# Two-layer cross-attention on one core: layer 2's keys and queries in two and a half blocks, and row maxima turned by one product

## The chip, the cores and the metric

The kernel runs on one core of a Trainium2 chip. The metric is the device time of one execution in microseconds (us): 1476.69 us is the median of three runs before the change (1475.23, 1476.69 and 1477.35 us).

The engines are named as in the profile. PE is the matrix engine, and PEld its weight load: each product loads a stationary operand and then streams a moving one past it. DVE is the vector engine, ACT the scalar engine, POOL the general engine, SP the engine that issues most of the transfers (DMAs). Each executes its own list of instructions in order; semaphores make one wait for another.

## The reference

Two layers follow each other on 16 batches of 256 positions with 320 channels, each with 20 heads of 16 channels. The context of a batch has 256 rows of 512 channels. Layer 1 takes its first 77 rows as text and the other 179 as image tokens; layer 2 takes the last 4 as image tokens and the other 252 as text. Cut to layer 2:

```python
q = heads(hidden_states @ W_q)
k_t = heads(text_ehs @ W_k)
scores_t = jnp.einsum('bhsd,bhtd->bhst', q, k_t) * attn_scale
probs_t = jax.nn.softmax(scores_t, axis=-1)
text_out = jnp.einsum('bhst,bhtd->bhsd', probs_t, v_t)
...
k_ip = heads(ip_ehs @ W_k_ip)
attn_scores = jnp.einsum('bhsd,bhnd->bhsn', q, k_ip) * attn_scale
qsem = jnp.einsum('bhst,bte->bhse', probs_t, text_ehs)
qsem = _l2norm(qsem)
sem = jnp.einsum('bhse,bne->bhsn', qsem, ip_n)
fused = attn_scores + SEM_SCALE * sem
probs_ip = jax.nn.softmax(fused, axis=-1)
probs_ip = probs_ip * spatial_mask[None, None, :, None]
ip_out = jnp.einsum('bhsn,bhnd->bhsd', probs_ip, v_ip)
...
out = out @ W_out + b_out
out = out + residual
```

`ip_n` are the normalised image tokens. All inputs and results are 32-bit floats.

## The kernel before, in words

**Halves.** PE multiplies in a rounded 32-bit type. To keep the accuracy, an operand is held as a high half (rounded, by ACT) and a low half (the remainder, by DVE or POOL), and a product is the sum of high by high, high by low and low by high: three products for each block of 128 contracted rows (`prod`). Queries contract 320 rows, two and a half blocks, with the half block's halves side by side in one block, so `project` has 8 products where a full count would be 9.

**Heads in 24 places.** The weights of queries and keys have their columns ordered by channel and head, 16 times 24 = 384 columns (`CP`), of which 20 of each 24 are heads. Layer 1 packs them to 320 (`CQ`). Layer 2 keeps 384: three whole blocks of 128 columns. `keys1` makes the keys of one batch, block by block (`m`), each with 4 x 3 products of 252 columns; `queries` with `project` makes the queries, each block with 8 products of 256 columns.

**Stacks.** Halves of keys and queries go through a scratch tensor in memory, `kd` and `qd`, with three copies of each channel row: keys low, high, high and queries high, low, high. `stacks1` loads, for each group of four heads, 48 rows (three copies of 16 channels) into `ks` and `qs`, two heads side by side in the upper and two in the lower half of the partitions, so that one product of 48 rows gives a score with all its halves. A 49th row of `ks` holds -1, and the same row of `qs` the row maximum, so the second, turned product gives the score less its maximum.

**Slots.** The work of one group of four heads is a slot: 80 slots of layer 1 (`slot0`), then 80 of layer 2 (`slot1`), five to a batch. In slot k of layer 2 `both1` is called for t = 0 and 1: the turned scores of group k into the banks T (line 917), the plain scores of group k+2 into bank S (line 922), the row maxima of these on DVE (line 923), and ACT's exponentials (line 929). Between the two, `attend1` makes the values' products of group k-2 into the single bank P (lines 988 and 990), which `settle1` reads; `norm1` makes the quadratic forms of group k-1 (line 975, the costliest group), and `rounded1` the halves of the probabilities (lines 965 and 966).

**Row maxima.** The maxima lie with positions on partitions, and are needed as a row. `maxima1` (line 955) and `maxima0` of layer 1 (line 780) turn them by two products with the unit matrix, one for each 128 positions, into a bank of the ring X. ACT copies the 4 or 8 rows of 256 numbers to `mt` (lines 957 and 782), and a DMA issued by ACT (line 959) carries them into the stacks. In layer 2 this stands at the end of slot k for group k+2.

**What sets the order.** A table, `STEPS`, says at which time, in slots, each step of the other work (keys "k1", queries "o1", tokens "t1", closing "c1" and "i1", weights "w1" to "w8") is put between the parts of the slots: `fill(k + part)` runs the steps that are due. PE's order is that of the calls throughout; in layer 2 that of ACT, DVE and POOL too. SP's order, and in layer 1 that of the others, is made by a scheduler from its own estimate of the times. `late` holds DVE's remainders and the DMAs behind them back between `hold` (before the last part of a slot) and `release` (before the second `both1`).

Of the kernel before, what the change touches and what calls it, by code (L numbers as in the profile page):

```python
# [16 lines left out]
B = 16  # L17
S = 256
# [15 lines left out]
KS1 = 49  # L34
XROW = 48

# [3 lines left out]
LEAD = 4  # L40

# [8 lines left out]
def xattn2(  # L50
# [101 lines left out]
    kd = [dram.tile([B // 2, 3, CQ, 2, S], F32, name="kd0"), dram.tile([B, 3, CP, 1, S], F32, name="kd1")]  # L152
# [81 lines left out]
    def weights(w_d, tag, half=None, wait=0, raw="raw"):  # L234

        w, parts, view = by_row(w_d, tag)
        yield from in_turn(parts, wait, raw)
        if half is not None:
            nc.vector.tensor_scalar_mul(w[:, 1, 2], f(w[:, 1, 2]), half)
        return view  # L240

# [105 lines left out]
    def keys_out(d, m, kst, b=slice(None)):  # L347

        for r, s in ((slice(1, 3), 0), (slice(0, 1), 1)):
# [130 lines left out]
    def weights7():  # L480
        cip = w1["cip"]
        image, wki1 = by_column(wki1_d)
        _, text, w1["k"] = by_row(wk1_d, "wA")
        yield from in_turn(image + text, 0.3, "rawc")
        for m in range(3):
            kp = bank()[:, :BI]
            prod(kp, lambda s, k: wki1(s, k, slice(m * 128, m * 128 + 128)), lambda s, k: cip[:, s, k], 4)
            halves(kip[:, 0, m], kip[:, 1, m], kp)
            yield

    def weights6():
# [15 lines left out]
        for i in range(2):  # L507
# [4 lines left out]
            v1t.append(v)  # L512
        yield

    def weights2():
        wq.append((yield from weights(wq1_d, "wE", tmask[:, 3:4], 0.3, "rawc")))
# [36 lines left out]
    def keys1(b):  # L553
        ct = ct1[b] = yield from context(b, 1, 0.3)
        for m in range(3):
# [4 lines left out]
            prod(kp, lambda s, k: w1["k"](s, k, ms), lambda s, k: ct(s, k)[:, :T1], 4)  # L560
# [4 lines left out]
                lambda kst=kst, m=m: keys_out(kd[1][b], m, kst),  # L565
# [60 lines left out]
    def project(l, w, a, evac):  # L626
# [9 lines left out]
    def queries(l, a):  # L636
# [6 lines left out]
        yield from project(l, wq[l], a, evac)  # L643
        qd = dram.tile([3, (CQ, CP)[l], S], F32, tag=f"qd{l}", name=f"qd{l}", bufs=2)
# [12 lines left out]
    def stack_rows(d):  # L657
        return d.rearrange("r (d h) t -> (r d) h t", d=D)

# [87 lines left out]
    def stacks1(k):  # L747
# [7 lines left out]
        for u in range(2):  # L755
            rows = slice(64 * u, 64 * u + XROW)
            hs = slice(4 * g + u, 4 * g + u + 3, 2)
            if k - NS < n:
                dma(K[64 * u + XROW : 64 * u + KS1], w1["ind"])
# [710 lines left out]
```

## Time and profile before

| | |
|---|---|
| median of three runs | 1476.69 us (1475.23 to 1477.35) |
| span of the profiled execution | 1475.7 us |
| what the median has beyond that span | 1.0 us (no time of the profiled execution is given apart from its span) |
| PE busy | 1433.6 us (97%), 12438 products |
| PEld busy | 1186.7 us (80%) |
| DVE, POOL, ACT busy | 1166.0, 1151.8, 956.5 us (79%, 78%, 65%) |
| DMA engines, mean busy share in slices | 0.1 to 0.7 |
| granted clock of PE, mean | 0.993 |

In a row of groups stand the line, the engine, the operation, the tiles (written <- read), the shapes and the count, then the busy time of the group, the mean duration of one in ns, and the idle time before them with what ended it. Products overlap: the mean of one (some 280 ns for 256 columns) is longer than what one adds to PE's time, which is the distance from its start to the next one's start. In a timeline row the first number is the start, the second the length in us, and a count at the end says how many instructions the row joins. Layer 1's slots fill the first 670 us or so, and layer 2's the rest.

### The profile page before, as it was taken

Reading aid. Unit: us, or ns where it says so; the run is one execution under the profiler, and the core shown is the slowest. Engines: PE = TensorE matmul, PEld = TensorE weight load, DVE = VectorE, ACT = ScalarE, POOL = GpSimd, SP = SyncE. Lnnn points to the kernel's source line nnn. Section 1 sums busy time; section 2 is a strip of 40 time slices with the busy share of each in tenths; the row PEclk is TensorE's granted clock in tenths of the full one; section 3 lists DMA queues with packets and bytes.
Section 4 is the critical chain, followed back from the end, with each engine's and each line's share of the span. In section 5 each row is a group of like instructions: output and inputs, shape, how many; then the busy total and the mean of one; then the engine's idle time right before and its main releaser. Section 6 shows DMA issues by size and latency. Waiting matters only on the chain.

```text
span 1475.7 us, 35302 instructions
## 1 busy us (share of the span) xinstructions
PE 1433.6 (97%) x12438; PEld 1186.7 (80%) x12438; DVE 1166.0 (79%) x2569; ACT 956.5 (65%) x2074; POOL 1151.8 (78%) x1173
## 2 busy tenths in 40 slices
PE   6899999999999999799999999999999999999998
PEld 6788888888888878687778887888888888888865
DVE  5487676777677787967888888888888888888897
ACT  5577676767676776756666566656665666566553
POOL 4179797979797877987788877787778877887785
PEclk9999999999999999999999999999999999999999
DMA  6756565656656577565434433543354345433511
GB/s 196 194 160 184 134 184 141 184 143 165 162 154 164 144 195 205 140 184 158 138 102 140 146 119 101 161 146 102 118 161 146 89 131 161 135 101 116 150 32 50
DMA packets 230667, 211.78 MB, mean 144 GB/s; under 512 B 56314, under 2 KB 217116, under 8 KB 230492
## 3 DMA queue, kind: packets, MB, share of 16 engines
q1 hardware_dynamic: 229222, 208.56, 50.3%
q8 instruction: 99, 1.62, 0.5%
q10 hardware_dynamic: 1270, 0.98, 0.2%
q14 instruction: 76, 0.62, 0.1%
HBM read 122.07 MB, written 86.44 MB: 141 GB/s over the span
## 4 chain that ended last, share of the span: by engine, by line
PE 86%; DMA 4%; DVE 3%; POOL 3%; ACT 2%; issue 1%; SPq 0%; ACTq 0%; DVEq 0%; POOLq 0%
PE X L260 22%; PE X L975 18%; PE X L632 11%; PE P L833 7%; PE S L772 5%; PE P L988 5%; PE T L917 5%; PE T L795 4%; PE S L922 3%; PE P L990 2%; DMA kd<-kst 2%; PE X L1108 1%; POOL P L801 1%; PE X L690 1%; POOL wt L966 1%
## 5 line engine op out<-in xcount | busy, mean ns | idle before, releaser
L801 POOL TENSOR_TENSOR P<-P,rs 128x512 f32<-128x512 f32 x320 | 413.6, 1316 | 140.2 <-ACT P L798 140.2
L975 PE MATMUL X<-ctb,gm 128*128 128x512 f32 x1120 | 295.3, 407 | 0.0
L966 POOL TENSOR_TENSOR wt<-P,ctb 128x512 f32<-128x512 f32 x212 | 268.6, 1296 | 0.0
L923 DVE TENSOR_REDUCE mn<-S 128x4 fp32r<-128x1008 f32 x160 | 192.8, 1205 | 81.0 <-PE S L922 79.4
L975 PEld LDWEIGHTS X<-ctb,gm 128*128 128x128 f32 x1120 | 203.6, 190 | 49.4 <-issue 0.4
L798 ACT ACTIVATE P<-T 128x512 f32<-128x512 f32 x320 | 174.7, 593 | 100.5 <-PE T L795 81.0
L978 DVE TENSOR_TENSOR wt<-X,wt 128x512 f32<-128x512 f32 x240 | 159.3, 681 | 4.9 <-PE X L975 4.9
L929 ACT ACTIVATE P<-T 128x512 f32<-128x512 f32 x212 | 115.0, 597 | 54.5 <-PE T L917 41.6
L980 POOL TENSOR_TENSOR wt<-wt 128x512 f32<-128x512 f32 x80 | 103.6, 1295 | 58.3 <-DVE wt L978 58.3
L965 ACT ACTIVATE ctb<-P 128x512 fp32r<-128x512 f32 x212 | 122.5, 625 | 32.7 <-PE X L975 31.1
L774 DVE TENSOR_REDUCE mn<-S 128x4 fp32r<-128x716 f32 x160 | 142.4, 890 | 0.0
L833 PE MATMUL P<-P,vr 128*32 128x256 f32 x1920 | 123.8, 387 | 1.8 <-DVE tmp L850 0.8
L632 PE MATMUL X<-hq,wE 128*128 128x256 f32 x768 | 111.1, 289 | 4.4 <-ACT hq L615 3.9
L260 PE MATMUL X<-cta,wA 128*128 128x252 f32 (+3 forms) x726 | 104.2, 289 | 6.9 <-ACT wA L187 6.8
L632 PE MATMUL X<-ho,wF 128*128 128x256 f32 x768 | 106.6, 284 | 0.9 <-DVE ho L871 0.6
L632 PEld LDWEIGHTS X<-hq,wE 128*128 128x128 f32 x768 | 101.6, 195 | 7.2 <-ACT hq L615 4.4
L260 PEld LDWEIGHTS X<-cta,wA 128*128 128x128 f32 (+1 forms) x726 | 94.4, 191 | 10.7 <-ACT wA L187 7.0
L632 PEld LDWEIGHTS X<-ho,wF 128*128 128x128 f32 x768 | 98.7, 189 | 3.9 <-DVE ho L871 1.0
L844 DVE STREAM_TRANSPOSE nt<-P 128x512 f32<-128x512 f32 x80 | 57.0, 713 | 44.2 <-PE P L833 43.9
L773 DVE TENSOR_REDUCE mn<-S 128x4 fp32r<-128x308 f32 x160 | 74.5, 466 | 21.5 <-PE S L772 21.1
L833 PEld LDWEIGHTS P<-P,vr 128*32 128x32 f32 x1920 | 55.7, 110 | 42.7 <-issue 6.0
L772 PE MATMUL S<-ks,qs 125*128 125x256 f32 x480 | 87.0, 304 | 0.9 <-DVE mn L774 0.8
(223 smaller groups left out, 3279.7 us busy)
## 6 DMA issues: line engine op xcount, KB each, us to landing
qd<-q SPq DMA_DIRECT2D x48, 384.0 KB
kd<-kst SPq DMA_DIRECT2D x66, 256.0 KB
rawc<-in_cT_dram SPq DMA_DIRECT2D x60, 256.0 KB
qs<-qd SPq DMA_DIRECT2D x160, 96.0 KB
ks<-kd SPq DMA_DIRECT2D x160, 96.0 KB
qs<-qd SPq DMA_DIRECT2D x60, 192.0 KB
ks<-kd SPq DMA_DIRECT2D x60, 192.0 KB
qd<-q SPq DMA_DIRECT2D x32, 256.0 KB
```

The source lines that it names most:

```text
L260: last = mm(out, lhs(a, k), rhs(b, k), start=i == 0, stop=i == len(terms) - 1)
L632: mm(pp, w(s, k, slice(m * 128, (m + 1) * 128)), a[:, t], start=i == 0, stop=i == len(terms) - 1)
L772: mm(sp[:, h], Q[: XROW + T0, h, t * 128 : (t + 1) * 128], K[: XROW + T0, h], start=True, stop=True)
L774: anchor(nc.vector.tensor_reduce(mn[:, t, 1], sp[:, :, T0:], axis=AX.X, op=ALU.max))
L798: exp = anchor(nc.scalar.activation(pt, st[p], AF.Exp, scale=SCALE))
L801: anchor(nc.gpsimd.tensor_mul(pt, pt, rs[:, t : t + 1].to_broadcast([128, 2, S])))
L833: mm(pv[32 * s : 32 * s + 32, o : o + S], v[:, vt, h : h + 32], P[k, s // 2][:, t, s % 2], start=vt < 2, stop=vt != 1,)
L923: anchor(nc.vector.tensor_reduce(maxes[k + 2][:, t], sp[:, :, :T1], axis=AX.X, op=ALU.max))
L965: nc.scalar.activation(R[k, u][:, t], P[k, u][:, t], AF.Copy, scale=0.5)
L966: anchor(nc.gpsimd.tensor_sub(W[k, u][:, t], P[k, u][:, t], f(R[k, u][:, t])))
L975: mm(yp, gm[:, gb], R[k, u][:, kt], start=i == 0, stop=i == len(blocks[n]) - 1)
L978: nc.vector.tensor_mul(product, yp, w[:, n])
```

## The change

**Layer 2's columns are packed to 320**, so the third block has 64 columns, and the other 64 columns of the block hold the low half of the weights' same columns (`both_halves`, by POOL, once). One product then gives high weights by the moving operand in its upper 64 rows and low weights in its lower 64 rows. Keys: 8 products for the third block in place of 12. Queries: 5 in place of 8. The lower 64 rows are not added to the upper: they are written to the scratch as rows of their own, and the stacks grow from 48 rows to 56 (`XR1`), with the row of -1 at 57. Each head has 8 more rows, of which 4 carry the keys' remainders against the queries' high half, and 4 the other way round; rows without a partner are zero (written once, in `weights6`).

**The scratch writes** are cut accordingly: for a batch 9 DMAs for the keys in place of 6, and 8 for the queries in place of 3. The loads of the stacks stay 4 to a group, of 56 rows in place of 48.

**The row maxima** are stored so that one product turns both halves of the positions: 16 rows of 128 numbers in layer 1, 8 in layer 2, in place of 8 and 4 rows of 256. In layer 2 the step moves from the end of slot k, for group k+2, to the middle of slot k behind the second `both1`, for group k+1, and its product goes into columns 384 to 511 of the values' bank P (77 of 80; three go to a bank of X).

**The image keys' weights** of layer 2 come in four loads by rows in place of three by columns.

**The table** moves to the head of the file; most times stay. "o1" has its fifth time at -5.4 (was -4), and a few times of weights, tokens and closings differ by up to 1.4 slots.

```diff
-KS1 = 49
 XROW = 48
+XR1 = 56
+KS1 = XR1 + 1
+C3 = 2 * 128
...
-        "o1": (-7, -6.8, -6, -5.8, -4, -3.4,),
+    "o1": (-7, -6.8, -6, -5.8, -5.4, -3.4,),
...
+    def both_halves(w):
+
+        for k in range(w.shape[2]):
+            nc.gpsimd.tensor_copy(w[:, 0, k, CQ:], f(w[:, 1, k, C3:CQ]))
...
+    def keys_out1(d, m, kst):
+
+        n = min(128, CQ - m * 128)
+        at = lambda q: slice(q * H + m * 128, q * H + m * 128 + n)
+        twice = d[16 * H : 48 * H].rearrange("(r p) t -> p r t", r=2)[m * 128 : m * 128 + n]
+        dma(twice, kst[:n, 0].unsqueeze(1).to_broadcast([n, 2, S]))
+        dma(d[at(0)], kst[:n, 1])
+        if m:
+            p = 112 * (2 - m)
+            dma(d[52 * H + 16 * (m - 1) : 52 * H + 16 * (m - 1) + n - p], kst[p:n, 0])
+        if m == 2:
+            dma(d[48 * H + 16 : 52 * H], kst[64:, 0])
...
+        none = v1t[0][:16, 0, 512:]
+        for c in range(2):
+            half = slice(128 * c, 128 * c + 128)
+            dma(kd[1][:, 48 * H : 48 * H + 16, half].rearrange("b p t -> p b t"), none.unsqueeze(1).to_broadcast([16, B, 128]))
+            for i in range(2):
+                dma(qd1[i][52 * H : 52 * H + 16, half], none)
...
-            prod(kp, lambda s, k: w1["k"](s, k, ms), lambda s, k: ct(s, k)[:, :T1], 4)
+            if m < 2:
+                prod(kp, lambda s, k: w1["k"](s, k, ms), lambda s, k: ct(s, k)[:, :T1], 4)
+            else:
+                for i in range(8):
+                    mm(kp, w1["k"](0, i // 2, ms), ct(i % 2, i // 2)[:, :T1], start=i == 0, stop=i == 7)
...
+            if packed and m == 2:
+                terms = [(0, 0, 0), (0, 0, 3), (0, 1, 1), (0, 1, 4), (0, 2, 2)]
...
-            for r, s in ((0, 0), (1, 1), (2, 0)):
-                dma(qd[r].rearrange("(m p) t -> p m t", p=128), qh[:, s])
+            whole = lambda q: qd[q * H : q * H + C3].rearrange("(m p) t -> p m t", p=128)
+            for q, s in ((0, 0), (16, 1), (32, 0)):
+                dma(whole(q), qh[:, s, :2])
+            dma(qd[: 48 * H].rearrange("(r p) t -> p r t", r=3)[C3:, ::2], qh[:64, 0, 2].unsqueeze(1).to_broadcast([64, 2, S]))
+            dma(qd[16 * H + C3 : 32 * H], qh[:64, 1, 2])
+            dma(qd[48 * H : 48 * H + 16], qh[112:, 0, 1])
+            dma(qd[48 * H + 16 : 52 * H], qh[:64, 0, 2])
+            dma(qd[52 * H + 16 :], qh[64:, 0, 2])
...
-        mp = bank()
-        for t in range(2):
-            mm(mp[:8, t * 128 : (t + 1) * 128], mn[:, t].rearrange("p a h -> p (a h)"), ident_r, start=True, stop=True)
-        mt = buf("mt", [8, S], FR)
-        casts.append(nc.scalar.copy(mt, mp[:8, :S]))
+        mp = bank()[:16, :128]
+        mm(mp, mn.rearrange("p a h t -> p (a h t)"), ident_r, start=True, stop=True)
+        mt = buf("mt", [16, 128], FR)
+        casts.append(nc.scalar.copy(mt, mp))
...
-    def maxima1(k):
+    def maxima1(k, into=None):
         mn = maxes[k]
-        mp = bank()
-        for t in range(2):
-            mm(mp[:4, t * 128 : (t + 1) * 128], mn[:, t], ident_r, start=True, stop=True)
-        mt = buf("mt", [8, S], FR)[:4]
-        nc.scalar.copy(mt, mp[:4, :S])
-        row = QK[k][0].rearrange("(u p) j t -> u p j t", u=2)[:, XROW]
+        mp = bank()[:8, :128] if into is None else into[:8, 384:]
+        mm(mp, mn.rearrange("p c t -> p (c t)"), ident_r, start=True, stop=True)
+        mt = buf("mt", [8, 128], FR)
+        nc.scalar.copy(mt, mp)
+        row = QK[k][0].rearrange("(u p) j t -> u p j t", u=2)[:, XR1]
         late(lambda: nc.scalar.dma_start(f(row), f(mt)))
...
         yield release
         yield lambda: both1(k, 1)
+        if k > NS:
+            yield lambda: maxima(k + 1, *[x[2] for x in summed])
...
         yield 0.8
-        yield lambda: maxima(k + 2)
         yield lambda: stacks(k + LEAD)
```

Over the whole program the lists differ, in PE, by 64 fewer products of keys (576 of 252 columns become 512), 48 fewer of queries (768 become 720) and 160 fewer of maxima (320 become 160). SP issues 135 more DMAs (1191 become 1326).

PE, one slot of layer 2 from its second `both1` to the next slot's first (T and S are the turned and plain scores, `gm` the operand of the quadratic forms, `hq` that of the queries, `ident_r,mn` the maxima, `wA` the keys). Before:

```order
L917 MATMUL T<-qs_188,ks_192 128x256 x4
L922 MATMUL S<-ks_190,qs_186 128x256 x4
L975 MATMUL X<-ctb_82,gm 128x512 x4
L632 MATMUL X<-hq_293,wE_85 128x256 x8
L975 MATMUL X<-ctb_82,gm 128x512 x3
L975 MATMUL X<-ctb_83,gm 128x512 x7
L955 MATMUL X<-ident_r,mn_555 4x128 x2
L260 MATMUL X<-cta_80,wA_84 128x252 x6
L260 MATMUL X<-cta_81,wA_84 128x252 x6
L917 MATMUL T<-qs_188,ks_192 128x256 x4
L922 MATMUL S<-ks_190,qs_186 128x256 x4
```

And in the changed kernel (line 1018 is what was 917, 1023 was 922, 1055 was 955, 1075 was 975, 725 was 632, 325 was 260):

```order
L1018 MATMUL T<-qs_190,ks_194 128x256 x4
L1023 MATMUL S<-ks_192,qs_188 128x256 x4
L1055 MATMUL P<-ident_r,mn_558 8x128
L1075 MATMUL X<-ctb_84,gm 128x512 x4
L725 MATMUL X<-hq_295,wE_87 128x256 x8
L1075 MATMUL X<-ctb_84,gm 128x512 x3
L1075 MATMUL X<-ctb_85,gm 128x512 x4
L725 MATMUL X<-hq_295,wE_87 128x256 x5
L1075 MATMUL X<-ctb_85,gm 128x512 x3
L325 MATMUL X<-cta_82,wA_86 128x252 x6
L325 MATMUL X<-cta_83,wA_86 128x252 x6
```

The maxima's product stands right behind the plain scores, into bank P, and the third block of the queries, now of 5 products, stands in this slot; before, its 8 products closed the next slot.

SP, the writes and loads of one batch of layer 2 (`kst` and `q` hold the halves of keys and queries, `kd` and `qd` are the scratch, `ks` and `qs` the stacks). Before:

```order
L83 DMA kd_67<-kst_235 128x2x256
L83 DMA kd_67<-kst_235 128x256
L83 DMA out_dram<-xc_747 128x3x256
L83 DMA qd_14293<-q_297 128x3x256 x2
L83 DMA xc_747<-x1d 128x3x256
L83 DMA qd_14293<-q_297 128x3x256
L83 DMA kd_67<-kst_236 128x2x256
L83 DMA kd_67<-kst_236 128x256
L83 DMA qs_188<-qd_14293 48x2x256 x4
L83 DMA qs_186<-qd_14293 48x2x256 x2
L83 DMA kd_67<-kst_235 128x2x256
L83 DMA kd_67<-kst_235 128x256
```

In the changed kernel, from the query loads of the same place on:

```order
L139 DMA qd_0_68<-q_299 64x256 x3
L139 DMA qs_190<-qd_0_68 56x2x256 x4
L139 DMA kd_67<-kst_237 128x2x256
L139 DMA kd_67<-kst_237 128x256
L139 DMA out_dram<-xc_747 128x3x256
L139 DMA xc_747<-x1d 128x3x256
L139 DMA qs_188<-qd_0_68 56x2x256 x2
L139 DMA kd_67<-kst_238 128x2x256
L139 DMA kd_67<-kst_238 128x256
L139 DMA kd_67<-kst_238 16x256
L139 DMA kd_67<-kst_237 64x2x256
L139 DMA kd_67<-kst_237 64x256 x3
```

All eight writes of the queries and the first four query loads now stand ahead of the first block of keys; between the last block of keys (four writes) and the key loads stand two query loads, as before.

ACT, around the maxima of one slot. Before:

```order
L957 CAST mt_196<-X 4x256
L959 DMA qs_187<-mt_196 2x2x256
L929 ACTIVATE P_95<-T 128x512
L929 ACTIVATE P_96<-T 128x512
L929 ACTIVATE P_95<-T 128x512
L929 ACTIVATE P_96<-T 128x512
L615 CAST hq_293<-xq_122 128x768
L965 ACTIVATE ctb_82<-P_95 128x512 x2
```

In the changed kernel (line 1030 was 929, 1065 was 965, 1057 was 957):

```order
L1030 ACTIVATE P_97<-T 128x512
L1030 ACTIVATE P_98<-T 128x512
L1030 ACTIVATE P_97<-T 128x512
L1030 ACTIVATE P_98<-T 128x512
L1057 CAST mt_198<-P 8x128
L1059 DMA qs_188<-mt_198 2x4x128
L1065 ACTIVATE ctb_84<-P_97 128x512 x2
```

The copy and the issue of its DMA moved from ahead of the slot's four exponentials to behind them, ahead of the halves of line 965. DVE's first read of bank P in `settle1` now also waits for this copy by ACT.

More of the change, by code (lines that the diff above doesn't have):

```diff
@@ L634, in project, with queries @@
             yield
-    def queries(l, a):
+    def queries(l, a, b=0):
         qh = buf("q", [128, 2, 3, S], FR)
@@ L995, in slot1 @@
         mine = k < 2 * NS
+        summed = []
         if k == NS:
@@ L1127, in open1 @@
         get("w2")
-        return (yield from queries(1, xs))[1]
+        return (yield from queries(1, xs, b))[1]
     results, tasks, delayed = {}, {}, []
@@ L1276, in ahead, with maxima @@
             both1(k - 2, t)
-    def maxima(k):
+    def maxima(k, *into):
         if k < 2 * NS:
-            (maxima0 if k < NS else maxima1)(k)
+            if k < NS:
+                maxima0(k)
+            else:
+                maxima1(k, *into)
     def part(*key):
```

107 lines of the change are left out of this document (63 added, 44 removed), and 58 rows, old and new, of the table STEPS.

## The prediction

> **What bounds the kernel now.** The first view is the page's head and its chain of waits.
>
> ```profile
> span 1475.7 us, 35302 instructions
> PE 1433.6 (97%) x12438; PEld 1186.7 (80%) x12438; DVE 1166.0 (79%) x2569; ACT 956.5 (65%) x2074; POOL 1151.8 (78%) x1173
> PE 86%; DMA 4%; DVE 3%; POOL 3%; ACT 2%; issue 1%; SPq 0%; ACTq 0%; DVEq 0%; POOLq 0%
> ```
>
> PE holds 86% of the chain. Since that is an average over stages, the second view is the table of stretches: the stretch, then busy time (and count) of PE, PEld, DVE, ACT and POOL, the granted clock, the DMA share and GB/s.
>
> ```profile
> 200.00:300.00 100.00, 99.78 (x943) 86.80 (x942) 73.51 (x184) 73.77 (x163) 86.22 (x77) 1.00 0.65 171
> 600.00:640.00 40.00, 33.92 (x337) 26.95 (x338) 33.00 (x72) 29.39 (x59) 37.03 (x34) 0.96 0.56 141
> 750.00:1400.00 650.00, 650.00 (x5479) 525.86 (x5478) 557.45 (x1166) 406.38 (x882) 517.71 (x565) 1.00 0.43 129
> ```
>
> Layer 1 keeps PE at 99.8%, the turn from one layer to the other leaves 6.1 of 40 us idle, and layer 2 shows PE without a gap for 650 us, with DVE at 557.45/650 = 86% as the next engine. A modelled end could hide waits in that 100%, so the third view is PE's waits from 740 us to the end. These are all of them (us in total, times, longest):
>
> ```profile
> PE P L990 <- DVE wt L980: 1.1, 1, 1.1
> PE X L1108 <- DVE rs L1100: 1.0, 1, 1.0
> PE S L922 <- DVE sr L939: 0.9, 2, 0.7
> PE X L632 <- DVE ho L871: 0.6, 2, 0.4
> PE P L990 <- POOL wt L980: 0.5, 1, 0.5
> PE P L988 <- DVE hsn L1044: 0.2, 1, 0.2
> ```
>
> 4.3 us in 736: in layer 2 nothing but PE's own list sets the pace, and a product that leaves it gives back the whole distance from its start to the next start. That distance is read from the fourth view, PE's timeline inside one batch:
>
> ```profile
> 1004.15 0.28 PE L955 MATMUL X<-ident_r,mn 128*4 128x128 f32 x2
> 1004.27 2.12 PE L632 MATMUL X<-ho,wF 128*128 128x256 f32 x16
> 1011.08 1.11 PE L632 MATMUL X<-hq,wE 128*128 128x256 f32 x8
> 1012.03 2.49 PE L975 MATMUL X<-ctb,gm 128*128 128x512 f32 x10
> 1023.06 1.54 PE L260 MATMUL X<-cta,wA 128*128 128x252 f32 x12
> 1024.44 0.28 PE L955 MATMUL X<-ident_r,mn 128*4 128x128 f32 x2
> 1024.56 1.16 PE L632 MATMUL X<-hq,wE 128*128 128x256 f32 x8
> ```
>
> **The change, part by part.**
>
> Keys: 12 products take 1024.44 - 1023.06 = 1.38 us, 0.115 us each. Four fewer a batch are 0.46 us, over 16 batches 7.4 us.
>
> Queries: 8 take 1012.03 - 1011.08 = 0.95 us, 0.119 us each. Three fewer are 0.36 us, over 16 batches 5.7 us.
>
> Maxima: a pair takes 1004.27 - 1004.15 = 0.12 us (and again 1024.56 - 1024.44), so one costs 0.06 us; 80 fewer in layer 2 are 4.8 us. The groups' rows bound it from above, those of both layers (the third row is line 955 in the 650 us of layer 2 alone):
>
> ```profile
> L780 PE MATMUL X<-ident_r,mn 128*8 128x128 f32 x160 | 24.8, 225 | 5.1 <-DVE mn L774 3.7 <-DMA kd<-kst 0.3 <-DVE ho L871 0.3
> L955 PE MATMUL X<-ident_r,mn 128*4 128x128 f32 x160 | 22.9, 223 | 0.6 <-DVE kst L564 0.6
> L955 PE MATMUL X<-ident_r,mn 128*4 128x128 f32 x132 | 18.6, 222 | 0.0
> PEld X L780 <- DVE mn L774: 7.4, 11, 1.7
> ```
>
> Busy time by count is 22.9/160 = 0.143 us, but that counts the overlap with the neighbour; the bounds for the 160 are 0 and 22.9 us, and the pair's distance is nearest since the stream stays as dense. In layer 1 the last row shows that 11 of 80 pairs wait for DVE's second half of the maxima. There the first product of the pair lay in the wait, and its removal is worth nothing: 69 x 0.06 = 4.1 us. The Trainium skill, "TensorE: Matmul & The Clock Gate", section "Back-to-back issue gap", gives some 81 ns for a product of 128 columns in a stream of load and product pairs; by that, as an estimate, the 149 would be worth 12.1 us instead of 8.9. The rows say 60 ns, so the measurement stands.
>
> Sum on PE: 7.4 + 5.7 + 4.8 + 4.1 = 22.0 us.
>
> The place of the maxima in layer 2: PE's product waits for nothing (its scores are a slot old, and bank P was filled just before by PE itself). What gets shorter is the row's way back to PE, since the next slot's first product needs it:
>
> ```profile
> 1018.11 0.50 PE L917 MATMUL T<-qs,ks 49*128 49x256 f32 x4
> 1018.65 1.09 ACT L929 ACTIVATE P<-T 128x512 f32<-128x512 f32 x2 [0.94 <-PE T L917]
> 1020.33 1.15 ACT L965 ACTIVATE ctb<-P 128x512 fp32r<-128x512 f32 x2 [0.58 <-PE X L975]
> 1020.70 0.44 DVE L1040 STREAM_TRANSPOSE nt<-P 128x256 f32<-128x256 f32 x1
> 1024.90 0.36 ACT L957 CAST mt<-X 4x256 fp32r<-4x256 f32 x1
> 1025.29 0.52 ACTq L959 DMA_DIRECT2D qs<-mt  x1
> 1025.65 0.51 PE L917 MATMUL T<-qs,ks 49*128 49x256 f32 x4
> ```
>
> The exponentials end at 1019.74. The copy (0.36 us or less, now 128 columns) and the issue (0.52, with 0.03 before it) bring it to 1020.65. Even a landing as slow as the writes below (2.5 us after the end of the issue) gives 1023.2, and the next slot asks at 1025.65: 2.5 us to spare where before there was a whole slot. So I cost it at nothing. ACT's line 965 starts at 1020.65 instead of 1020.33; what hides those 0.3 us is ACT itself, idle a third of the time, and that the halves made here are read by PE only in the next slot. If this cover went, 80 slots would lose 0.3 us each, 24 us. `settle1` on DVE now waits for the copy, over at 1020.1; before, DVE came to it at 1020.70: nothing.
>
> SP: 8 more DMAs for a batch. Its timeline for the batch whose first plain scores stand in the last row here:
>
> ```profile
> 1030.03 0.44 SPq L83 DMA_DIRECT2D qd<-q  x1
> 1030.57 1.45 SPq L83 DMA_DIRECT2D kd<-kst  x2
> 1034.40 2.82 SPq L83 DMA_DIRECT2D qs<-qd  x6
> 1037.33 0.89 SPq L83 DMA_DIRECT2D kd<-kst  x2
> 1038.31 0.87 SPq L83 DMA_DIRECT2D qs<-qd  x2
> 1040.69 4.06 SPq L83 DMA_DIRECT2D ks<-kd  x8
> 1033.48 0.38 DVE L564 TENSOR_TENSOR kst<-X,kst 128x252 fp32r<-128x252 f32 x1
> 1046.06 0.51 PE L922 MATMUL S<-ks,qs 48*128 48x256 f32 x4
> ```
>
> The key loads wait for the last key writes: 1040.69 less the writes' end 1038.22 is 2.5 us of landing. The first two of the eight loads end their issue at 1041.7, land by the same 2.5 us at 1044.2, and are needed at 1046.06: 1.9 us to spare, the tightest place of the batch. The last keys are ready at 1033.86, and their writes go out only at 1037.33, because SP stands until 1034.40 waiting for the queries' last write (1030.03) to land and then issues six loads. With the third block of queries a slot earlier, all eight writes go out from about the time of the first key block, some 10 us sooner, and that wait is over before the last keys are made. Four key writes at 0.45 us (0.89 for two above) from 1033.9 end at 1035.7 and land at 1038.2. The two query loads ahead of the key loads still wait for their buffer, as at 1038.31, so the key loads start near 1039.2: earlier by 1.5 us, not later. Cost nothing; if all 8 extra issues (0.45 us each, 3.6 us) came in between, they would exceed the 1.9 us, which is a rival below.
>
> Once only: seven small copies by POOL to pack the weights, six DMAs of zeros, one more weight load.
>
> ```profile
> L304 POOL CAST wA<-wB 128x64 fp32r<-128x64 f32 x8 | 2.4, 319 | 1.9 <-ACT wB L187 1.4 <-DVE wB L188 0.5
> ```
>
> 7 x 0.32 = 2.2 us of POOL, which has 3 of 40 us free in the stretch 600 to 640, and 7 x 0.45 = 3.2 us of SP: between 0 and 5.4 us, and since this lies beside PE's 6.1 idle us there, I take 1. The first two batches' keys and queries are made in that turn too, where a product less can end in a wait: of 2 x 0.82 us I count half as lost, 0.8. The retimed steps could move those 6.1 us either way, by up to 4, as far as the quoted rows show; taken as 0.
>
> Result: 22.0 - 1 - 0.8 = 20.2 us off the span, 1475.7 to 1455.5. The median of the runs lies 1.0 us above the span, so **1456.5 us**.
>
> **Rivals.**
>
> *Half of it comes back as new waits.* DVE has 557.45 us of work in 650; the new pace, 635 us for the same work (132 maxima products in 650 us, ten to a batch, are 13.2 batches of 49 us, each shorter by 0.46 + 0.36 + 0.30 = 1.12 us), leaves it 88% busy. S is one bank, DVE's reduction of the first scores must be over before the second, and the maxima's copy now stands in ACT's way. Were half lost: 1475.7 - 10 + 1 = 1466.7. Against it: the waits above are 4.3 us in all.
>
> *The retimed turn helps beyond the sum.* If 4 of the 6.1 idle us go and the setup is hidden: about 1451.5.
>
> *No change.* If PE's 100% were only the model of its ends, PE would have room and another chain would set the pace: 1476.7. The Trainium skill, "Perfetto Trace Analysis", section "Identifying the Most-Contended Engine", says that matmul busy time is a bad measure and the share of weight loads a good one. The rows give that share as 525.86/650 = 81%, so by this rule PE would have a fifth to spare; no run here has yet told which holds. Against it: no engine is busier than 86% and hardly any wait is left on PE. It also covers that the new products cost what the old ones did.
>
> *Slower: the key loads arrive late.* Place: SP's list ahead of the first `ks` loads of each batch. If the eight extra issues (3.6 us) delay them, 1.9 us are covered, the shorter batch takes 1.1 more, and PE waits 2.8 us a batch, 42 us over 15 batches: 1456.5 + 42 = 1498. It decides from 1.4 us a batch on, where it eats the 22 us. For it: 135 more issues on an in-order queue with waits for landings. The Trainium skill, "DMA: Bandwidth & Descriptors", section "Rules for kernel authors", says that transfers below 64 KB are mostly overhead, which speaks against writes cut into 16 and 64 rows. Against it: in the new order only the key writes, two more of them, fall between the last keys and the loads.
>
> **How the numbers follow.** Forecast 73%, half 13%, more 7%, no change 3%, slower 4%. The forecast's own range, from the costs 0 to 5.4 and the maxima by 0.143 us at most, with some of that in waits, is 1449 to 1462. To leave out no more than 2 in 10 the range takes in the half case: 1447 to 1468. What a measurement can tell from no change is 0.2%, 3 us. Faster by more than that: 73 + 13 + 7 = 93%; within 3%; slower 4%.
>
> **What would show it.** Right: PE's stretches of layer 2 still at 100%, a batch of five slots 1.1 us shorter, one maxima product at some 0.06 us, DVE near 88%, the key loads issued before 1.9 us of the need. Wrong: a row "PE T <- DMA qs<-mt" (the maxima's row late), "PE S <- DMA ks<-kd" (the keys late), DVE's or ACT's waits on each other growing into PE rows, or more than 8 idle us in PE between the layers.

## The result, and the profile after

The changed kernel takes 1452.62 us (median of 4 runs, 1451.59 to 1459.92) against 1477.02 before: a ratio of 0.9848, 95% interval 0.9825 to 0.9871. A second series, put among the experiments below, gave 1453.99 and 0.9856 (0.983 to 0.9882). Forecast was 1456.5. The profiled execution took 1451.59 us.

The head of the page of the changed kernel:

```profile
span 1449.8 us, 35042 instructions
PE 1401.7 (97%) x12166; PEld 1157.8 (80%) x12166; DVE 1174.2 (81%) x2570; ACT 937.6 (65%) x2075; POOL 1152.3 (79%) x1181
```

The span is 25.9 us shorter, where 20.2 were forecast. The same three kinds of stretch as before (busy us and counts of PE, PEld, DVE, ACT, POOL; clock, DMA share, GB/s):

```profile
200.00:300.00 100.00, 100.00 (x932) 86.48 (x934) 74.78 (x183) 72.08 (x162) 86.88 (x78) 1.00 0.66 176
600.00:640.00 40.00, 32.37 (x317) 25.32 (x317) 32.81 (x67) 25.45 (x52) 34.36 (x35) 1.00 0.69 172
750.00:1380.00 630.00, 629.43 (x5315) 507.99 (x5316) 562.01 (x1165) 394.76 (x876) 518.45 (x565) 1.00 0.47 137
```

Layer 2 still has PE almost without a gap (629.43 of 630 us), and DVE is now at 562.01/630 = 89%. PE's waits from 715 us to the end are these (us in total, times, longest), with no DMA among them:

```profile
PE P L1090 <- DVE wt L1080: 2.3, 2, 1.3
PE S L1023 <- DVE sr L1040: 2.3, 5, 0.8
PE X L1209 <- DVE rs L1201: 1.0, 1, 1.0
PE X L1075 <- DVE wt L1078: 0.7, 1, 0.7
PE X L725 <- DVE ho L972: 0.6, 2, 0.4
PE P L1090 <- POOL wt L1080: 0.4, 1, 0.4
PE P L1088 <- DVE hsn L1145: 0.2, 1, 0.2
```

From slot 15 of layer 2 to the end they sum to 4.5 us, as against 4.3 before: on PE's own list the change brought no new waits there.

**Where the time went** is read from one mark, the start of PE's first plain scores of a slot. In PE's timeline of before, these are the marks of layer 2 for slots 15 and 75, twelve batches apart (the counts are cut by the window):

```profile
797.82 0.40 PE L922 MATMUL S<-ks,qs 48*128 48x256 f32 x3
1393.64 0.40 PE L922 MATMUL S<-ks,qs 48*128 48x256 f32 x3
```

and in that of the changed kernel:

```profile
789.79 0.40 PE L1023 MATMUL S<-ks,qs 56*128 56x256 f32 x4
1367.56 0.39 PE L1023 MATMUL S<-ks,qs 56*128 56x256 f32 x4
```

A batch took (1393.64 - 797.82)/12 = 49.65 us and takes 48.15: 1.50 us less, where 1.12 were forecast. Marked the same way, layer 1 goes from 7.538 to 7.425 us a slot (slots 20 to 60): 0.11 less, where 0.05 were forecast. But from slot 60 of layer 1 to slot 15 of layer 2 only 1.3 us are gained. There PE's work fell by 6.6 us while its idle time grew from 294.70 - 280.51 = 14.2 to 293.40 - 273.89 = 19.5 us. That stretch before, and then in the changed kernel:

```profile
503.10:797.80 294.70, 280.51 (x2504) 229.76 (x2503) 239.19 (x514) 195.98 (x425) 240.47 (x230) 0.98 0.57 162
```

```profile
496.40:789.80 293.40, 273.89 (x2442) 222.98 (x2442) 240.13 (x515) 191.16 (x424) 239.95 (x237) 0.99 0.61 166
```

So the forecast's total is close, but three of its parts are off. The experiments ask which.

### The profile page after: what moved, and what is told of

Its sections match the earlier page's. It is cut to its first block, busy times and chain, and to the rows that moved or that the text cites. A ratio compares the mean times of both kernels' runs of the same rounds, so it can differ in the third digit from the quotient of the medians.

```text
span 1449.8 us, 35042 instructions
## 1 busy us (share of the span) xinstructions
PE 1401.7 (97%) x12166; PEld 1157.8 (80%) x12166; DVE 1174.2 (81%) x2570; ACT 937.6 (65%) x2075; POOL 1152.3 (79%) x1181
## 4 chain that ended last, share of the span: by engine, by line
PE 52%; DVE 3%; POOL 1%; issue 1%; ACT 0%; DMA 0%; ACTq 0%; DVEq 0%; POOLq 0%
PE X L1075 18%; PE X L325 9%; PE X L725 6%; PE P L1088 5%; PE T L1018 4%; PE S L1023 3%; PE P L1090 2%; PE X L1209 1%; PE X L651 1%; PE P L1055 1%; DVE mn L1024 1%; PE P L934 1%; POOL P L902 0%; DVE wt L1078 0%; POOL wt L1066 0%
## 5 line engine op out<-in xcount | busy, mean ns | idle before, releaser
L725 PE MATMUL X<-hq,wE 128*128 128x256 f32 x720 | 102.7, 286 | 4.6 <-ACT hq L706 3.3
L725 PEld LDWEIGHTS X<-hq,wE 128*128 128x128 f32 x720 | 96.4, 193 | 8.3 <-ACT hq L706 3.8
L874 PEld LDWEIGHTS S<-ks,qs 125*128 125x128 f32 x480 | 64.4, 189 | 28.2 <-issue 24.1
L325 PE MATMUL X<-cta,wA 128*128 128x252 f32 (+3 forms) x534 | 78.8, 292 | 7.9 <-ACT wA L244 5.7
```

The costliest lines, as they stand in the source:

```text
L325: last = mm(out, lhs(a, k), rhs(b, k), start=i == 0, stop=i == len(terms) - 1)
L725: mm(pp, w(s, k, slice(m * 128, (m + 1) * 128)), a[:, t], start=i == 0, stop=i == len(terms) - 1)
L874: mm(sp[:, h], Q[: XROW + T0, h, t * 128 : (t + 1) * 128], K[: XROW + T0, h], start=True, stop=True)
```

## The experiments

All are made from the changed kernel unless told otherwise. The two slopes of each trace (by the marks above) stand beside its time; "ratio" is to the kernel before.

| kernel | layer 1, us a slot | layer 2, us a batch | median us | ratio, 95% interval |
|---|---|---|---|---|
| before | 7.538 | 49.65 | 1477.02 | 1 |
| changed | 7.425 | 48.15 | 1452.62 | 0.9848 (0.9825 to 0.9871) |
| changed, once more | 7.424 | 48.16 | 1453.99 | 0.9856 (0.983 to 0.9882) |
| layer 2's product twice | 7.426 | 48.42 | 1460.55 | 0.9894 (0.9878 to 0.991) |
| layer 1's product twice | 7.475 | 48.15 | 1457.24 | 0.9871 (0.9855 to 0.9886) |
| layer 2's product at the old place | 7.424 | 48.59 | 1460.89 | 0.989 (0.987 to 0.9909) |
| blocks with the old number of products | 7.426 | 48.97 | 1464.59 | 0.9924 (0.9908 to 0.9939) |
| layer 2's third query block as late as before | 7.427 | 48.55 | 1457.85 | 0.988 (0.9863 to 0.9898) |
| whole old table of steps | 7.525 | 48.54 | 1463.01 | 0.9909 (0.9894 to 0.9924) |
| old steps in the turn alone | 7.424 | 48.19 | 1455.66 | 0.9862 (0.9847 to 0.9877) |
| before, with the new table | 7.473 | 49.60 | 1478.78 | 0.9999 (0.9987 to 1.0011) |
| no maxima product in layer 2 | 7.427 | 48.17 | 1456.68 | 0.9852 (0.9835 to 0.987) |
| layer 1's product behind the values | unsteady | 48.14 | 1476.64 | 1.0 (0.9983 to 1.0018) |

**What may be read from a slope: the changed kernel once more.**

> The changed kernel itself once more, word for word, to tell what of the differences above is the kernel's and what is the execution's. If the slopes are the kernel's: layer 1 from slot 20 to 60 at 7.42 us a slot and a batch of layer 2 at 48.15 us again, to 0.03 us, while the start, the turn and the total move by up to 4 us. If the slopes move from execution to execution by more than 0.1 us a batch, the readings by slope above (0.06 us for a product, 0.4 us for the place) don't hold. Total: 1451 to 1456.

Both slopes came again, to 0.01 us, and the span was 0.5 us longer. The other kernels agree: those without an edit in the steady slots of layer 1 lie there at 7.424 to 7.427 us, those without one in the steady batches of layer 2 at 48.14 to 48.19. A slope therefore belongs to the kernel, as far as these traces go, and tells apart what a median, with runs up to 8 us apart, does not; less than 0.05 us a batch is not read from it. The slopes carry what follows; the medians are the check on the sum.

**The price of one small product: twice in layer 2, twice in layer 1.**

```diff
-        mm(mp, mn.rearrange("p c t -> p (c t)"), ident_r, start=True, stop=True)
+        for again in range(2):
+            mm(mp, mn.rearrange("p c t -> p (c t)"), ident_r, start=True, stop=True)
```

> The changed kernel, but in layer 2 the one product that turns the row maxima is issued twice in the same place, into the same bank (repeated work only; same result). 80 products more, of the very kind that the change took away, in a stream that keeps PE busy without a gap. Theory A (the price in the dense stream, 60 to 63 ns from start to next start, as the pairs show): +5 us, 1457.6, and a batch of layer 2 longer by 0.3 us. Rival B (each such small product costs 0.14 us with what it does to its neighbours, as the surplus of the change over the forecast suggests: 1.5 us a batch instead of 1.1): +11 us, 1463.8, a batch longer by 0.7 us. Rival C (the two products hide in other work): 0.

A batch is longer by 0.28 us, five products of 0.055. PE's timeline shows the two:

```profile
848.26 0.28 PE L1056 MATMUL P<-ident_r,mn 128*8 128x128 f32 x2
848.38 1.84 PE L1076 MATMUL X<-ctb,gm 128*128 128x512 f32 x7
```

0.12 us for both, as the pair had before. By the slope theory A stands and rival B falls. The median rose by more than the forecast 5 us (7.9). The profiled execution lost 3.3 us once in layer 1, of which below; whether the other three did is not on record.

The same edit in layer 1:

> The changed kernel, but in layer 1 the one product that turns the row maxima is issued twice in the same place (repeated work only; same result): 80 products more in layer 1. Theory A (60 ns each): +4.8 us, 1457.4, the start of the plain scores of slot 60 of layer 1 later by 3.6 us than in the changed kernel's trace (496.4). Rival B (0.115 us each, as the change gained per slot there): +9 us, 1461.8, slot 60 later by 6.9 us.

0.05 us a slot and +4.6 us: theory A again. Slot 60 alone would not have told: it came 5.0 us later (501.4 against 496.4), between the two theories, since 3.0 of that were lost before slot 20, where the slopes begin. So the forecast's price of a product was right in both layers, and the surplus of 0.4 us a batch and 0.06 us a slot comes from something else.

**The two blocks.**

```diff
+                for i in (0, 1, 2, 3):
+                    mm(kp, w1["k"](0, i // 2, ms), ct(i % 2, i // 2)[:, :T1], start=i == 0, stop=i == 3)
                 for i in range(8):
                     mm(kp, w1["k"](0, i // 2, ms), ct(i % 2, i // 2)[:, :T1], start=i == 0, stop=i == 7)
...
+            if packed and m == 2:
+                for i, (s, k, t) in enumerate(terms[:3]):
+                    mm(pp, w(s, k, slice(m * 128, (m + 1) * 128)), a[:, t], start=i == 0, stop=i == 2)
```

> The changed kernel with the products that it took from the third blocks put back as repeated work ahead of them: four more for a batch's keys (252 columns), three more for its queries (256 columns). The writes, loads and packed weights stay as in the changed kernel; same result. Theory A (keys and queries gave what the forecast says: 16 x (4 x 0.115 + 3 x 0.119) = 13.1 us): 1465.7, a batch longer by 0.8 us. Rival B (they carried part of the surplus, that is the gain of a batch, 1.5 us, but for 0.3 of maxima): +19 us, 1471.8, a batch longer by 1.2 us. Rival C (the packed rows, loads and writes gained or lost something of their own, hidden in the sum): then e4 lies at neither.

A batch is longer by 0.82 us, just the 0.46 + 0.36 of the forecast, and the time by 12.0. Together with the doubled product this also settles the rival "no change": work that is given back to PE costs its full distance, so PE's own list does set the pace of layer 2. By the rule of the Trainium skill, "Perfetto Trace Analysis", section "Identifying the Most-Contended Engine", PE's weight loads (507.99/630 = 81%) would have left it room; these two runs decide against it here.

**The place of the product in layer 2.**

```diff
         yield lambda: both1(k, 1)
-        if k > NS:
-            yield lambda: maxima(k + 1, *[x[2] for x in summed])
...
         yield 0.8
+        yield lambda: maxima(k + 2)
         yield lambda: stacks(k + LEAD)
```

> The changed kernel with layer 2's one product for the maxima back at the old place, the end of the slot, for the group two slots ahead, into a bank of X of its own; number of products unchanged. Theory A (what the change gained beyond the forecast in layer 2, 0.4 us a batch or some 6 us, came from the new place, because at the old place the product stood ahead of the transposed scores or between neighbours of other shapes): +4 to +7 us, 1457 to 1460, a batch of layer 2 longer by 0.3 to 0.4 us. Rival B (the place is free and the products themselves cost more than the forecast has): within 2 us of the changed kernel, 1451 to 1454.5. Rival D (the old place is better, since the row's way back to PE is longer there): 1448 to 1451.

A batch is longer by 0.44 us: theory A, though both the batch and the time (1460.89) are a little above its ranges. The edit moves the place, the bank (X instead of P) and the group (k+2 instead of k+1) together, and no run tells these three apart. PE's timeline shows two things at the old place.

First, the product costs its own 0.06 us there, also right ahead of the next slot's turned scores. From the first product of the keys to the turned scores it is 868.98 - 867.44 = 1.54 us in this kernel,

```profile
867.44 1.55 PE L325 MATMUL X<-cta,wA 128*128 128x252 f32 x12
868.83 0.22 PE L1055 MATMUL X<-ident_r,mn 128*8 128x128 f32 x1
868.98 0.50 PE L1018 MATMUL T<-qs,ks 57*128 57x256 f32 x4
```

and 866.61 - 865.14 = 1.47 us in the changed kernel, which has no product between them:

```profile
865.14 1.54 PE L325 MATMUL X<-cta,wA 128*128 128x252 f32 x12
866.61 0.51 PE L1018 MATMUL T<-qs,ks 57*128 57x256 f32 x4
```

Second, once a batch the turned scores stand. From their start to the plain scores it is then 888.83 - 888.23 = 0.60 us in this kernel,

```profile
888.23 0.87 PE L1018 MATMUL T<-qs,ks 57*128 57x256 f32 x4
888.83 0.51 PE L1023 MATMUL S<-ks,qs 56*128 56x256 f32 x4
```

and 0.34 us at the same point of the changed kernel's batch:

```profile
885.76 0.50 PE L1018 MATMUL T<-qs,ks 57*128 57x256 f32 x4
886.10 0.40 PE L1023 MATMUL S<-ks,qs 56*128 56x256 f32 x4
```

In each of 13 batches of this trace (790 to 1376 us) the second weight load of these scores starts 0.05 us after DVE has ended `ho` (line 972), and the profile puts the wait down to it. The kernel before has it too, in each of 12 batches there (DVE's `ho` is line 871 in it); the changed kernel has it in none. Why these scores have to wait for DVE there was not looked into. Five times 0.06 and once 0.26 are 0.56 us a batch; the 0.12 beyond the measured 0.44 come back elsewhere in the batch.

What it costs at the new place is told by leaving it out:

```diff
-        mm(mp, mn.rearrange("p c t -> p (c t)"), ident_r, start=True, stop=True)
         mt = buf("mt", [8, 128], FR)
-        nc.scalar.copy(mt, mp)
+        nc.scalar.copy(mt.rearrange("p (r n) -> p r n", n=8), f(mn[:8].rearrange("p c t -> p (c t)")).unsqueeze(1).to_broadcast([8, 16, 8]))
```

> The changed kernel without layer 2's product for the maxima: ScalarE fills the row from eight rows of the maxima themselves, repeated, so the maxima that are taken off are not those of their own rows; everything else, copy, row and DMA, stays. It tells what the single product costs at its new place, between the plain scores and the quadratic forms. Theory A (there it costs next to nothing: without a small product between them the first quadratic form behind the scores takes 0.34 us to the next, with it 0.28 and the product 0.063, so 5 to 10 ns net): a batch of layer 2 within 0.06 us of the changed kernel's 48.15, the total within 2 us of it. Rival B (it costs its own 63 ns): a batch shorter by 0.3 us, 1447 to 1448.

The batch did not get shorter: 48.17 us against 48.15 with the product. At its new place the product is free. (The median is 4 us longer than the changed kernel's, outside theory A's 2 us; in the profiled execution, the longest of the four, the trace puts most of that into layer 1, ahead of the edit, below.) PE's timeline shows how; first the changed kernel, then this one:

```profile
840.09 0.48 PE L1023 MATMUL S<-ks,qs 56*128 56x256 f32 x4
840.50 0.23 PE L1055 MATMUL P<-ident_r,mn 128*8 128x128 f32 x1
840.57 1.83 PE L1075 MATMUL X<-ctb,gm 128*128 128x512 f32 x7
842.24 0.59 PE L1209 MATMUL X<-rs,rs 128*128 128x256 f32 x2
```

```profile
848.41 0.50 PE L1023 MATMUL S<-ks,qs 56*128 56x256 f32 x4
848.84 1.89 PE L1074 MATMUL X<-ctb,gm 128*128 128x512 f32 x7
850.57 0.59 PE L1208 MATMUL X<-rs,rs 128*128 128x256 f32 x2
```

From the plain scores, which use 56 of the 128 rows, to line 1209 it is 842.24 - 840.09 = 2.15 us with the product and 850.57 - 848.41 = 2.16 without. The seven quadratic forms take 1.67 us behind the product and 1.73 right behind the scores: the first product on all rows behind products on some of them costs about 0.06 us more, and whichever product comes first pays that. The small one is as long as what it saves the next.

**The steps.** First the one number of the third block of queries:

```diff
-    "o1": (-7, -6.8, -6, -5.8, -5.4, -3.4,),
+    "o1": (-7, -6.8, -6, -5.8, -4, -3.4,),
```

> The changed kernel with one number of its table put back: the queries' third block of layer 2 at step -4 instead of -5.4, that is about one and a half slots later, nearer to the keys' writes. Theory A (the earlier place is what keeps SP's longer list clear of the key loads, as the prediction's term on SP says; with the later one the wait for the queries' last writes stands again ahead of the last key writes and the loads slip by 1.5 us or more): the first key loads of a batch in steady layer 2 less than 1.5 us ahead of the need, PE rows that wait for ks<-kd, up to 2.8 us a batch, so 1455 to 1490. Rival B (SP has room for its 135 more issues in either order, no row of PE waits for them): within 2 us of the changed kernel, 1451 to 1455, slope of layer 2 unchanged at 48.2 us a batch.

Neither theory had it. A batch is longer by 0.40 us, and not through late keys. The first key loads of the batch whose plain scores stand in the second row start 5.1 us ahead of it in the changed kernel,

```profile
1025.45 3.40 SPq L139 DMA_DIRECT2D ks<-kd  x8
1030.59 0.41 PE L1023 MATMUL S<-ks,qs 56*128 56x256 f32 x4
```

and 4.9 us in this one:

```profile
1027.99 3.40 SPq L139 DMA_DIRECT2D ks<-kd  x8
1032.91 0.40 PE L1023 MATMUL S<-ks,qs 56*128 56x256 f32 x4
```

What is new is among the waits of PE's weight loads from 790 to 1370 us, a row that neither the kernel before nor the changed one has there:

```profile
PEld X L325 <- DVE wt L1078: 9.0, 24, 0.6
```

Two times a batch a weight load of the keys' products (`X<-cta,wA`) waits 0.4 us, by the profile for a bank of X that DVE still reads. PE's own starts show the loss where the row says: between the last quadratic form and the keys' first product it is 0.38 us on average instead of 0.23, twice a batch, and the keys' products themselves take 0.11 us a batch more, 0.41 in all. That wait is the kind which the prediction's rival "half of it comes back as new waits" named (DVE at 88%, its waits growing into PE's). The earlier step avoids it.

Then the whole old table (with `v0e` and `s0o`, the values and scores of layer 1, among 13 changed entries):

```diff
-    "v0e": (-7, -5.2, -4.8,),
+    "v0e": (-7, -5.4, -5,),
-    "s0o": (-2.4, -1.4, -1, -0.8, -0.4, 0.4, 1.6,),
+    "s0o": (-2.4, -1.4, -1, -0.8, -0.4, 0, 1.2,),
...
```

> The changed kernel with the whole old table of steps; products, rows and places as in the changed kernel. Layer 1: the change gained 0.115 us a slot there and one product is worth 0.06, so half is open. Theory A (the retimed values and scores of layer 1 took away two waits of 0.3 us a batch, the pair waiting for DVE's second half and the transposed scores): layer 1 longer by 0.05 to 0.06 us a slot, the start of slot 60 at 499 to 500 instead of 496.4. Rival B (the waits fell because the second product of the pair is gone): slot 60 within 0.7 us of 496.4. The turn between the layers: PE stood 19.5 us in the changed kernel and 14.2 before; if the retimed steps made that, the old ones give back about 5 us there; if it is the missing work of PE itself (its products went, the others' chain did not), nothing. Total: 1449 to 1457.

Layer 1 is longer by 0.10 us a slot, layer 2 by the same 0.40 us a batch, and the changed kernel loses 10 us of its 24: 1463.01. The time misses the expected 1449 to 1457. For layer 1 theory A has the direction and half the size (0.05 to 0.06; slot 60 came at 500.3). For the turn the run says that the new steps didn't make the idle time there: with the old ones it lasts longer (slot 60 to slot 15: 297.9 us against 293.4, of which 3.2 are the two slopes').

From the other side, the kernel before with the new table alone:

> The kernel before with the new table of steps and nothing else (products, rows, writes and the place of the maxima as before). Theory A (the retimed values and scores of layer 1 are a gain of their own, 0.08 us a slot, as the old table cost the changed kernel; the later steps of layer 2 are only needed by the shorter batch, whose slope was 0.4 us a batch longer with the old one, while the batch before shows no such wait): layer 1 shorter by 0.08 us a slot from slot 20 to 60, 3.2 us there and some 5 to 6 in all, layer 2 unchanged at 49.65 us a batch: 1470 to 1472. Rival B (the steps of layer 1 gain only together with the single product): 1476 to 1478. Rival C (the earlier third block of queries also helps the batch before): a batch of layer 2 shorter by up to 0.4 us, 1465.

Layer 1 gained 0.064 us a slot, a little less than theory A's 0.08, and layer 2 next to nothing (49.60). The waits of PE's weight loads from 200 to 480 us show what went. Before:

```profile
PEld X L780 <- DVE mn L774: 1.4, 4, 0.3
PEld X L260 <- PE X L709: 0.9, 3, 0.3
```

Neither row is left with the new table. But the time as a whole did not follow, and is above theory A's 1470 to 1472: 0.9999, though the profiled execution (span 1472.1) was 3.6 us shorter than that of before. It was the fastest of 12. In its trace the stretch from slot 60 to slot 15 took 1.4 us more than before, so part was lost there again; where the other runs lost the rest the trace of one cannot tell, so that the table is a gain in the kernel before is not shown; that it is one in the changed kernel is.

The products and the table also depend on one another. With the old table one product fewer gives layer 1 0.013 us a slot (7.538 to 7.525), with the new one 0.05 (7.473 to 7.425): where the pair waited for DVE's maxima, the saved product went into the wait.

The turn's steps alone:

```diff
-    "w1": (-20.6, -20.4, -19.4, -18.8, -18.8, -18.6, -18,),
+    "w1": (-21.4, -20.4, -19.4, -18.8, -18.8, -18.6, -18,),
-    ("w3", 1): (0.2,),
+    ("w3", 1): (1.6,),
...
```

> The changed kernel with the old steps for the tasks of the turn alone (the weights' loads w1, w6, w3, w8 and the first batch's queries), the new ones everywhere else. If the new steps of the turn cost the 5 us that PE stands longer there: 1447 to 1449, faster than both. If PE stands longer only because it has less to do while the chain of the other engines is as long as before: 1451 to 1454, and PE's idle time between the layers near 19 us as now.

1455.66: no gain (and 1.7 us above the second expectation), the turn differs by 0.4 us, and PE's idle time in it is 19.0 us as against 19.5. So the turn did not keep its length through these steps. That it kept it because PE had less to do and the other engines as much as before fits (in the stretch above DVE, ACT and POOL are within 5 us of what they were), but no run shows it. PE's waits from 560 to 740 us in the changed kernel begin with

```profile
PE X L881 <- ACT wE L244: 2.1, 2, 1.3
PE X L325 <- ACT P L899: 1.7, 1, 1.7
PE T L1018 <- DVE ho L972: 1.5, 2, 0.8
PE X L881 <- ACT cta L244: 1.5, 1, 1.5
```

and go on like that, 18 rows in all, no one of which holds the 5 us. Which chain of the others bounds the turn stays open.

**A free place in layer 1?**

```diff
-            yield lambda: maxima(k + 1)
             yield lambda: stacks(k + LEAD - 1, "M")
...
             yield lambda: attend0(k - 1)
+            yield lambda: maxima(k + 1)
             yield lambda: stacks(k + LEAD - 1, "T")
```

> The changed kernel with layer 1's one product for the maxima moved in its slot from ahead of the scores to behind the products of the values (128x32), ahead of the second half's scores. If a small product is free where PE changes from products on a part of its rows or columns to whole ones, as in layer 2, this place is free too: the first score behind the values takes 0.223 us to the next there, 0.117 elsewhere, and the score behind the product at the old place 0.170. Theory A: 0.05 to 0.11 us a slot less, 4 to 9 us, 1444 to 1449. Rival B (the switch behind the values costs the product as well): 0 to -4 us. Rival C (the row is late, since it has 4 us instead of 7 until the next slot's first turned scores; rows PE T <- DMA qs<-mt): slower than the changed kernel, 1455 or more.

Rival C decides: 1476.64, all of the change's gain gone. From slot 10 to 20 the slots were 0.09 us shorter, within theory A, but then the row came late. PE's waits from 130 to 560 us:

```profile
PE T L896 <- DMA qs<-mt: 6.3, 6, 2.4
```

Most was lost toward the turn, where the last slots of layer 1 (60 to 77) took 149 us instead of 131; of these 18 us the same row has 7.3 from 560 to 672 us, in three waits. Slots 10 to 20 look as if the place were free for PE; no longer stretch shows it. A free place is worth nothing where the row that comes of it is needed 4 us later.

## Why the prediction was right, and where it was not

The total, 3.9 us beside the forecast, owes part of its closeness to luck: the terms that follow were off by up to 7 us, and not all one way.

**The bound.** Right. PE's list sets the pace of layer 2; the products of the blocks and the second copies, put back, cost their distance.

**Keys and queries**, 13.1 us: right to 0.01 us a batch (0.82 measured). That the new products cost what the old ones did holds with it.

**The maxima's price**, 0.06 us: right in layer 2 (0.055 in the doubled run) and layer 1 (0.05), and rightly not the 0.143 of busy time by count. That the first product of a pair was hidden where the pair waited for DVE is what layer 1 shows with the old table, only more so: 0.013 us a slot were left of it.

**The place of the maxima**, "I cost it at nothing": the term that was mis-sized. It looked only at what a late row could cost, and was right there (no wait for `qs<-mt` in layer 2). What it left out is that the one product which stays costs its 0.06 us at the old place and nothing at the new one, and that at the old place the turned scores stand for DVE once a batch: 0.44 us a batch in all, 7.0 us over 16. The wait was there in the kernel before, in a slot that the prediction's timeline of PE has not; from the scores' start to the mark 1393.64 it is 0.58 us instead of 0.34:

```profile
1393.06 0.85 PE L917 MATMUL T<-qs,ks 49*128 49x256 f32 x4
```

PE's list of waits, on which the prediction rested, does not have it either, since there the weight load waits while PE still counts as busy. With 0.82 for the blocks, 0.28 for the second product (priced at the new place) and 0.44 for the place the parts give 1.54 of the 1.50 measured.

**The steps**, "taken as 0": wrong. The prediction looked for their effect only in the turn, where they have next to none in the changed kernel. In layer 1 they are worth 0.064 us a slot, 5 us by 80 slots; in layer 2 they keep 0.40 us a batch, 6.4 us by 16, from being lost to a bank that DVE reads. With the old table the change is worth 13 us, near the 10 of the rival "half comes back as new waits": that rival named the right engine, though another bank (X, not S), and the table is why it didn't come. With the old table a batch gains 49.65 - 48.54 = 1.11 us, the very 1.12 of the forecast, but by chance: the 0.44 of the place and the 0.40 of the new wait cancel.

**Setup and turn**, 1.8 us: too little. By the slopes, the 20 slots of layer 1 and three batches of layer 2 between the marks should have gained 20 x 0.113 + 3 x 1.50 = 6.8 us, and 1.3 came: 5.5 us went into PE's idle time, which grew by 5.3. In the stretch from 600 to 640 us itself it is 7.6 us, just below the 8 named as a sign. But a fixed stretch holds other work in the faster kernel; between the marks the idle time was above 8 before the change already, so that sign told nothing.

**SP.** The eight writes more cost nothing, as said, but not because the key loads start 1.5 us earlier: they start 5.1 us ahead of the need, where it was 1046.06 - 1040.69 = 5.4 us before. No row of PE waits for them.

The 5.7 us that the span lost beyond the forecast's 20.2 are thus 6.1 for layer 2 (0.38 us a batch beyond the 1.12, from the place) and 5.0 for layer 1's steps, which the sum lacked, less 3.7 that the turn kept beyond the forecast's 1.8 and 1.7 at the end: the last five slots, where a batch's rate would have given 1.5 us, gained nothing.

## What to carry to other kernels

Price a small product by the distance from the start before it to the start behind it, with it and without it, at its old place and at its new one: here it cost 0.06 us at the one and nothing at the other, behind products on some of the rows and ahead of products on all of them. Then look a few products further and at the waits of the weight loads: the old place also made the turned scores stand 0.26 us once a batch, and PE's own list of waits had no row for it. Where one engine is busy without a gap, take products back and double them to read prices from slopes: over twelve equal batches they came again to 0.01 us, and to 0.05 across kernels with the same batch, while whole runs differ by some us. And when work leaves the bounding engine, look at once for the next engine's late reads of a bank, and give the steps back their distance, or part of the gain turns into waits.

## What the runs showed of the hardware

A product on 8 columns that costs PE nothing behind products on 56 rows (48.17 us a batch without it, 48.15 with it) was not expected. Nor was this: in the doubled run of layer 2 and in the run without the product, both without an edit in layer 1, one and the same vector instruction took 4.93 us once, where its median is 1.02 us; the row is from the doubled run's DVE timeline.

```profile
130.14 4.93 DVE L709 SCALAR_TENSOR_TENSOR hq<-hq,tmask,xq 128x256 fp32r<-128x256 f32 x1
```

PE then stood 3.3 us in both, and the layer 1 of these two executions stayed some 4 and 6 us behind the changed kernel's to its end. No other trace but these two shows it; its cause was not looked for.
